# A graph-attention kernel with its slots laid out anew: score blocks and weighted sums in pairs, the dense work in one block, two small operations moved from VectorE to ScalarE

## Chip, cores and metric

One core of a Trainium2 chip. The metric is the device time of one execution in microseconds (us). Times are medians of several executions. Single executions of one kernel differ by up to 0.5%.

## The reference, cut to what matters

32 graphs of 512 nodes with 256 features go through two layers, each with a residual and a norm:

```python
# layer 0: masked attention (8 heads of 32) + feed-forward
allowed = (adj > 0) | (swapaxes(adj, 1, 2) > 0) | eye
attn = softmax(where(allowed, (q * scale) @ k.T, -inf));  ctx = attn @ v
x1 = layernorm(x + ctx @ Wo.T + bo)
ff = relu(x1 @ W1.T + b1) @ W2.T + b2
x  = layernorm(x + layernorm(x1 + ff))
# layer 1: masked attention alone, the mask is adj != 0 removed
x  = layernorm(x + (attn1 @ v1) @ Wo1.T + bo1)
```

All in float32.

## The kernel before

A graph and layer is one slot; 64 slots run one after the other. A slot works on eight blocks k of 128 keys x 4 heads x 512 queries (k = 0 to 3 are heads 0 to 3, k = 4 to 7 heads 4 to 7). These are the pieces that the argument touches (cuts marked):

```python
def scores(self, layer, k):                 # "S": four score matmuls, array form 32*128
    s = ps_s.tile([P, HPC, N], F32, tag="s")             # four PSUM banks, one buffer
    ...  # nc.tensor.matmul(s[:, j, :], kT, qT)
    p = work.tile([P, HPC, N], F32, tag="p", bufs=8)
    nc.scalar.activation(p, s, AF.Exp, scale=SCALE)      # "Exp"
def masked(self, layer, k):                 # "mask", on VectorE
    nc.vector.tensor_tensor(p, p, m[...].to_broadcast([P, HPC, N]), ALU.mult)
def product(self, k):                       # "P": weighted sum, array form 128*32, into psA
    ...
    if kc == NQ - 1:
        if hg == 0: self.tile("cT", [ND, N], bufs=1)     # context, ONE buffer
        nc.scalar.copy(self.cT[:, hg, :], self.acc[hg])
def pair(self, k):                          # p[k] += p[k+1], an accumulating DMA issued by GpSimd
    nc.gpsimd.dma_start(out=self.p[k], in_=self.p[k + 1], accum_op=ALU.add)
def fold(self, dst, a, b):                  # p[dst] = p[a] + p[b], on VectorE
def sums(self, k, hg, first, last):         # "R": row sums by TensorE, psR, form 128*32
```

Everything else on TensorE (projections, transposes, feed-forward, the masks of the next graphs) has the dense form 128*128; its results share two PSUM banks ("d") and mostly leave by ScalarE. In PSUM, masks of layer 0 (psM) left by VectorE and masks of layer 1 (psN) by ScalarE. In the names below, `project` is the output projection, `out0` and `out1` take the statistics for the norm after it, `norm1` to `norm4` apply the norms, and `hidden` and `mlp` are the two layers of the feed-forward. The slot beside a feed-forward began and went on like this:

```python
def slot_forward(g, layer, last, later, rest):
    g.scores(layer, 0)
    ...
    g.scores(layer, 1); g.masked(layer, 0)
    last.project(0, 0); last.project(0, 1); last.out0(0); last.out0(1)
    g.scores(layer, 2); g.masked(layer, 1); g.product(0); g.pair(0)
    g.query_key(layer, 1, 1)
    last.norm1(0); last.norm1(1); last.out0(2); last.out0(3)
    g.scores(layer, 3); g.masked(layer, 2); g.product(1)
    last.transpose(last.x1, 0); last.norm1(2); last.norm1(3)
    g.scores(layer, 4); g.masked(layer, 3)
    last.hidden(0, 0); last.hidden(0, 2)
    last.transpose(last.x1, 1); last.residual1()
    g.product(2); g.pair(2)
    g.scores(layer, 5); g.masked(layer, 4)
    last.hidden(0, 4); last.hidden(0, 6); g.product(3)
    ...
```

The order within each engine is the order of this program.

## Time and profile before

| | before |
|---|---|
| time | 3380.41 us (3379.92 to 3380.94, 3 runs) |
| TensorE busy | 98% |
| VectorE, ScalarE busy | 78%, 50% |
| slots O1, F1, F2, O2 | 40.2, 64.75, 64.0, 39.5 us; 16 groups of 208.4 us |
| mean granted TensorE clock | 0.997 |

A slot is measured from its S0 to the next S0. O1 is layer 0 of the first graph of a pair (beside it stand the last output projections of the pair before and the masks of the graphs to come), F1 layer 0 of the second graph (beside the feed-forward of the first), F2 layer 1 of the first, O2 layer 1 of the second. The prediction below shows the page's busy line and chain, and stretches of the timelines. The waits of TensorE (what waited, for what: us in total, times, longest), of the kernel before:

```profile
PE psS L273 <- ACT p L277: 13.4, 34, 1.0
PE psR L314 <- DVE p L307: 11.9, 31, 0.4
PE psA L290 <- DVE p L282: 5.7, 7, 4.0
```

TensorE waits almost nowhere: 31 us in the three largest entries. Next the view by windows, for one stretch of 3.41 us (the length, then the busy time of TensorE, its weight loads, VectorE, ScalarE and GpSimd, each with its number of instructions, then the granted clock, the DMA share and GB/s):

```profile
1021.83:1025.24 3.41, 3.41 (x21) 1.92 (x21) 2.96 (x3) 2.09 (x4) 0.38 (x1) 1.00 0.90 302
```

### The profile page before, as it was taken

The numbers are of one execution on the slowest core, as the hardware profiler recorded it, in microseconds if no ns is written. First come the engines' busy times: TensorE is split into PE (matmuls) and PEld (weight loads), VectorE is DVE, ScalarE is ACT, GpSimd is POOL, SyncE is SP. The second block draws the span as 40 slices with busy tenths as digits, with TensorE's granted clock in tenths as the row PEclk, the third lists the DMA queues.
The fourth block names the chain that finished last, engine by engine and source line by source line (L and its number), as shares of the span: only waits on it lengthen the run. The fifth ranks groups of instructions, "written<-read, shape, count | busy, mean of one in ns | idle before, by whom it ended". The sixth has DMA issues, their size and how long they took to land.

```text
span 3379.3 us, 47797 instructions
## 1 busy us (share of the span) xinstructions
PE 3321.8 (98%) x19210; PEld 1808.0 (54%) x19210; DVE 2620.6 (78%) x3525; ACT 1684.5 (50%) x1921; POOL 1111.7 (33%) x1641
## 2 busy tenths in 40 slices
PE   8999999999999999999999999999999999999997
PEld 3655546455464554645546455564655645555464
DVE  5787787878878777787777877778777787877877
ACT  4454454545545455454554544545445455444543
POOL 2333333233333333323333233332423323333232
PEclk9999999999999999999999999999999999999999
DMA  7454555545645455464554645536455365454643
GB/s 173 88 106 100 94 113 100 103 91 105 116 86 115 87 109 108 82 125 83 111 100 86 128 86 110 101 83 125 85 110 100 82 125 97 97 100 91 120 77 70
DMA packets 169670, 343.83 MB, mean 102 GB/s; under 512 B 10081, under 2 KB 144353, under 8 KB 144865
## 3 DMA queue, kind: packets, MB, share of 16 engines
q0 software_dynamic: 112128, 285.24, 46.9%
q1 hardware_dynamic: 57312, 55.46, 5.0%
q8 instruction: 153, 2.51, 0.3%
q14 instruction: 77, 0.62, 0.1%
HBM read 72.23 MB, written 16.78 MB: 26 GB/s over the span
## 4 chain that ended last, share of the span: by engine, by line
PE 85%; DVE 9%; ACT 4%; DMA 1%; issue 1%; POOL 0%; SPq 0%; POOLq 0%; DVEq 0%
PE psS L273 16%; PE psH L380 14%; PE psF L398 13%; PE psA L290 11%; PE psV L243 6%; PE psQK_None L260 6%; PE psO L359 6%; DVE p L282 4%; ACT p L277 4%; PE psQK L260 4%; PE psR L314 3%; PE psT L231 2%; DVE p L307 2%; PE psM L206 1%; PE psN L218 1%
## 5 line engine op out<-in xcount | busy, mean ns | idle before, releaser
L282 DVE TENSOR_TENSOR p<-p,m 128x2048 f32<-128x2048 f32 x512 | 1164.7, 2281 | 51.4 <-ACT p L277 51.3
L277 ACT ACTIVATE p<-psS 128x2048 f32<-128x2048 f32 x512 | 961.5, 1878 | 470.7 <-PE psS L273 433.6
L337 POOL TENSOR_SCALAR rs<-mv 128x1 f32<-128x1 f32 x512 | 376.4, 735 | 1223.9 <-DVE mv L336 1205.5
L273 PE MATMUL psS<-qT,kT 32*128 32x512 f32 x4096 | 583.9, 640 | 15.9 <-ACT p L277 13.4
L290 PE MATMUL psA<-p,v 128*32 128x512 f32 x4096 | 539.7, 605 | 5.7 <-DVE p L282 5.7
L380 PE MATMUL psH<-xT,w_L_gnn_W 128*128 128x256 f32 x2048 | 467.7, 384 | 0.0
L398 PE MATMUL psF<-w_L_gnn_W,hT 128*128 128x256 f32 x2048 | 455.9, 381 | 0.0
L380 PEld LDWEIGHTS psH<-xT,w_L_gnn_W 128*128 128x128 f32 x2048 | 381.2, 190 | 123.3 <-issue 51.1
L388 ACT ACTIVATE hT<-psH,c_L_gnn_b 128x256 f32<-128x256 f32 x512 | 214.6, 470 | 430.5 <-PE psH L380 429.4
L398 PEld LDWEIGHTS psF<-w_L_gnn_W,hT 128*128 128x128 f32 x2048 | 384.0, 190 | 73.9 <-ACT cT L300 24.3
L338 POOL TENSOR_TENSOR rs<-rs,neg_half 128x1 f32<-128x1 f32 x512 | 306.4, 598 | 42.7
L273 PEld LDWEIGHTS psS<-qT,kT 32*128 32x128 f32 x4096 | 159.9, 182 | 273.1 <-issue 199.4
L307 DVE TENSOR_TENSOR p<-p,p 128x2048 f32<-128x2048 f32 x128 | 292.6, 2286 | 4.1 <-DMA p<-p 1.8
L304 POOL DMA_DIRECT2D p<-p x192 | 182.3, 949 | 263.3 <-PE psV L243 174.9
L260 PE MATMUL psQK_None<-xT,w_L_gnn_Wqkv 128*128 128x512 f32 x512 | 254.6, 620 | 3.3 <-DMA w_L_gnn_Wqkv<-in_L_gnn_Wqkv_dram 3.3
L359 PE MATMUL psO<-w_L_gnn_Wo,cT 128*128 128x256 f32 x1024 | 248.6, 391 | 0.5 <-DVE held L829 0.5
L250 ACT COPY v<-psV 128x512 f32<-128x512 f32 x128 | 74.9, 585 | 347.6 <-PE psV L243 347.6
L359 PEld LDWEIGHTS psO<-w_L_gnn_Wo,cT 128*128 128x128 f32 x1024 | 188.0, 191 | 98.0 <-issue 63.3
L324 POOL TENSOR_TENSOR total<-total,sT 128x16 f32<-128x16 f32 x128 | 37.5, 293 | 574.8 <-DVE sT L321 574.8
L314 PE MATMUL psR<-p,ones 128*32 128x512 f32 x1536 | 198.0, 601 | 13.9 <-DVE p L307 11.9
L290 PEld LDWEIGHTS psA<-p,v 128*32 128x32 f32 x4096 | 84.0, 108 | 234.6 <-issue 84.8
L321 DVE STREAM_TRANSPOSE sT<-psR 128x512 f32<-128x512 f32 x128 | 91.5, 715 | 151.0 <-PE psR L314 151.0
(74 smaller groups left out, 3308.7 us busy)
## 6 DMA issues: line engine op xcount, KB each, us to landing
p<-p POOLq DMA_DIRECT2D x192, 1024.0 KB, 7.7
x<-in_x_dram SPq DMA_DIRECT2D x64, 512.0 KB, 4.3
x<-bov POOLq DMA_DIRECT2D x64, 512.0 KB, 5.8
adj<-in_adj_dram POOLq DMA_DIRECT2D x32, 512.0 KB, 6.9
x<-s_L_gnn_ln_b POOLq DMA_DIRECT2D x32, 512.0 KB, 7.9
x<-s_L_gnn_b POOLq DMA_DIRECT2D x32, 512.0 KB, 5.6
out_dram<-x SPq DMA_DIRECT2D x32, 512.0 KB, 3.0
w_L_gnn_W<-in_L_gnn_W_dram SPq DMA_DIRECT2D x2, 1024.0 KB, 12.6
```

Of the source, the lines that this page charges most:

```text
L260: nc.tensor.matmul(ps, w[:, i, c * P : (c + 1) * P], self.xT[:, i, at], start=(i == 0), stop=(i == ND - 1))
L273: nc.tensor.matmul(s[:, j, :], self.kT[at, hg, kc * P : (kc + 1) * P], self.qT[at, hg, :], start=True, stop=True)
L277: nc.scalar.activation(p, s, AF.Exp, scale=SCALE)
L282: nc.vector.tensor_tensor(p, p, m[:, k % NQ, None, :].to_broadcast([P, HPC, N]), ALU.mult)
L290: nc.tensor.matmul(self.acc[hg][j * HD : (j + 1) * HD, :], self.v[:, kc, h * HD : (h + 1) * HD], self.p[k][:, j, :], start=(kc == 0), stop ...
L307: nc.vector.tensor_tensor(self.p[dst], self.p[a], self.p[b], ALU.add)
L314: nc.tensor.matmul(self.total[j * HD : (j + 1) * HD, :], ones, self.p[k][:, j, :], start=first, stop=last)
L337: nc.gpsimd.tensor_scalar(rs, mv[:, 1:2], EPS, None, ALU.add)
L338: nc.gpsimd.tensor_tensor(rs, rs, neg_half[:, 0:1], ALU.pow)
L359: nc.tensor.matmul(ps[:, j, :], self.cT[:, k, at], wo[layer][:, k, :], start=(k == 0), stop=(k == ND - 1))
L380: nc.tensor.matmul(ps[:, j, :], w1[:, c, at], self.xT[:, c, h * 2 * P : (h + 1) * 2 * P], start=(c == 0), stop=(c == ND - 1),)
L398: nc.tensor.matmul(ps, self.hT[h][:, f, j * P : (j + 1) * P], w2[:, f, :], start=(f == 0), stop=(f == NF - 1))
```

## The change

The intent: a change of the array's form costs TensorE time, and in the kernel before it changed form 1781 times. So each slot is laid as four rounds of scores, a pair of weighted sums, scores, and one dense block. To relieve VectorE, the masks of layer 0 are taken by Sign on ScalarE, and the last norm is applied on ScalarE, with an offset -mean*rstd made on GpSimd. The core of the diff, with cuts marked:

```diff
-                nc.vector.tensor_scalar(self.m0[:, i, :], ps, 0.0, None, ALU.is_gt)
+                nc.scalar.activation(self.m0[:, i, :], ps, AF.Sign)
...
+                ms = small.tile([P, 1], F32, tag="ms", name=f"ms_{self.b}_{n}_{i}")
+                nc.gpsimd.tensor_scalar(ms, mv[:, 0:1], rs, -1.0, ALU.mult, ALU.mult)
+                return ms, rs
...
-                nc.vector.tensor_scalar(self.x2[:, i, :], y, mean, rs, ALU.subtract, ALU.mult)
+                nc.scalar.activation(self.x2[:, i, :], y, AF.Identity, bias=ms, scale=rs)
... opening of a slot that follows an O slot: P6, P7 and their row sums come from the slot before
+            elif last:
+                last.product(6)
+                last.product(7)
+                last.sums(3, 1, first=True)
+                last.sums(4, 1, last=True)
+            g.scores(layer, 1)
... F slots
             g.scores(layer, 2)
-            g.masked(layer, 1)
             g.product(0)
+            g.product(1)
             g.pair(0)
-            g.query_key(layer, 1, 1)
...
             g.scores(layer, 3)
-            g.masked(layer, 2)
-            g.product(1)
-            last.transpose(last.x1, 0)
             last.norm1(2)
             last.norm1(3)
+            g.masked(layer, 2)
+            g.masked(layer, 3)
+            g.query_key(layer, 1, 1)
...
+            last.transpose(last.x1, 0)
             g.scores(layer, 4)
-            g.masked(layer, 3)
-            last.hidden(0, 0)
-            last.hidden(0, 2)
+            g.product(2)
+            g.product(3)
+            g.scores(layer, 5)
+            g.masked(layer, 4)
+            g.masked(layer, 5)
             last.transpose(last.x1, 1)
             last.residual1()
-            g.product(2)
             g.pair(2)
-            g.scores(layer, 5)
...
+            for f in range(0, NF, 2):
+                last.hidden(0, f)
             last.mlp(0)
+            last.mlp(1)
             g.fold(2, 2, 0)
... O slots in the same way; the last graph's second projection now comes after S5 in O1:
+            g.scores(layer, 5)
+            g.masked(layer, 4)
+            if new:
+                new.value(0, 0)
+            if last and not forward:
+                last.project(1, 1)
```

## The prediction

> **What bounds the kernel now.** I read the page first (shares of the engines, then the chain that ended last), then the timelines of TensorE, VectorE and ScalarE over slots in the steady middle. The program is 64 slots. Each slot computes eight score blocks S0 to S7 of one graph and layer, their Exp, their masks and their weighted sums P0 to P7, and puts the dense work of another graph between them.
>
> ```profile
> PE 3321.8 (98%) x19210; PEld 1808.0 (54%) x19210; DVE 2620.6 (78%) x3525; ACT 1684.5 (50%) x1921; POOL 1111.7 (33%) x1641
> ...
> PE 85%; DVE 9%; ACT 4%; DMA 1%; issue 1%; POOL 0%; SPq 0%; POOLq 0%; DVEq 0%
> ...
> L282 DVE TENSOR_TENSOR p<-p,m 128x2048 f32<-128x2048 f32 x512 | 1164.7, 2281 | 51.4 <-ACT p L277 51.3
> L277 ACT ACTIVATE p<-psS 128x2048 f32<-128x2048 f32 x512 | 961.5, 1878 | 470.7 <-PE psS L273 433.6
> ...
> L307 DVE TENSOR_TENSOR p<-p,p 128x2048 f32<-128x2048 f32 x128 | 292.6, 2286 | 4.1 <-DMA p<-p 1.8
> ```
>
> TensorE is the bound: it is hardly idle and carries 85% of the chain. VectorE is second at 78%, so whether it delays TensorE is a matter of order, not of total.
>
> ```profile
> 1000.01 1.06 PE L290 MATMUL psA<-p,v 128*32 128x512 f32 x8
> 1000.89 1.04 PE L314 MATMUL psR<-p,ones 128*32 128x512 f32 x8
> 1001.87 7.17 PE L380 MATMUL psH<-xT,w_L_gnn_W 128*128 128x256 f32 x32
> ...
> 1036.35 1.07 PE L290 MATMUL psA<-p,v 128*32 128x512 f32 x8
> 1037.35 1.98 PE L260 MATMUL psQK_None<-xT,w_L_gnn_Wk 128*128 128x512 f32 x4
> ```
>
> The first column is the start. A weighted sum takes 0.88 us when a block of the same array form (128*32) follows, and 1.00 us when another form follows. Over all matmuls of the trace, the medians from start to start are: dense 256-column 216 ns, but 309 ns before another form; last matmul of a 128*32 block 409 ns, but 522 ns before another form. A score block takes 1.07 us whatever follows. So leaving the dense form costs 93 ns and leaving the 128*32 form 113 ns.
>
> Measured from each slot's S0 to the next one's, slots repeat in groups of four per pair of graphs: O1 40.2, F1 64.7, F2 64.0, O2 39.5 us (O: beside output projection and masks; F: beside the feed-forward); 16 groups of 208.4 us are 3334 us, and head and tail make the rest.
>
> **What the Trainium skill says.** "TensorEngine Tiling (Array Packing)", Key Properties: "Changing tiling mode (not just tile) drains the TensorE". The trace agrees, with 93 and 113 ns. "TensorE: Matmul & The Clock Gate", architectural detail on queue depths: matmuls and the instructions of ScalarE and VectorE keep their order, and only weight loads are pulled ahead. The trace agrees: VectorE sits idle 2.40 us in the next fence behind a psO that is not ready, though nothing else is missing. "ScalarE: Activation LUTs", What ACT_TABLE_LOAD costs: about 186 ns + 0.833 ns per element with immediates, for every function, and 93 ns more per pointer operand. The mask copy of layer 1 (128x512) takes 602 ns here, against 613 by that sum; so I take 0.60 us for Sign, and estimate 186 + 186 + 213 = 0.58 us for the norm with two pointers. The built program has one table load, as before.
>
> **The change, part by part.** The built order of TensorE's instructions holds the same matmuls, but 1117 changes of array form in place of 1781. Exits from dense fall from 759 to 319 (440 x 93 ns = 41 us), exits from 128*32 from 510 to 288 (222 x 113 ns = 25 us), exits from scores stay about 512. **Gain: 66 us, 4.1 us per group.** Sign and norm take 87 + 50 us from VectorE and put 77 + 74 us on ScalarE; neither is the bound, so only their place in the queues counts. P6, P7 and two row sums of a slot move to the next slot's opening: no work added.
>
> The cost is waits, since the regrouping asks for masked blocks sooner. I follow each slot in the built order with the durations above.
>
> F slots: VectorE must do, in this order, the statistics of out0(0), out0(1), mask 1, norm1, out0(2), out0(3), norm1, masks 2 and 3. Here is that stretch before, from the timeline of VectorE and then of TensorE:
>
> ```profile
> 1115.98 0.42 DVE L348 TENSOR_TENSOR y<-psO,x 128x256 f32<-128x256 f32 x1 [2.40 <-PE psO L359]
> ...
> 1117.98 2.27 DVE L282 TENSOR_TENSOR p<-p,m 128x2048 f32<-128x2048 f32 x1
> ...
> 1124.26 2.26 DVE L282 TENSOR_TENSOR p<-p,m 128x2048 f32<-128x2048 f32 x1
> ...
> 1128.53 4.49 DVE L282 TENSOR_TENSOR p<-p,m 128x2048 f32<-128x2048 f32 x2
> ...
> 1129.34 0.60 PE L231 MATMUL psT<-ident,x 128*128 128x128 f32 x4
> 1129.87 1.07 PE L290 MATMUL psA<-p,v 128*32 128x512 f32 x8
> 1130.87 1.14 PE L273 MATMUL psS<-qT,kT 32*128 32x512 f32 x8
> 1131.94 3.72 PE L380 MATMUL psH<-xT,w_L_gnn_W 128*128 128x256 f32 x16
> 1135.59 1.06 PE L290 MATMUL psA<-p,v 128*32 128x512 f32 x8
> ```
>
> From 1115.98 to the end of mask 3 (the first of the two at 1128.53) are 14.8 us without a gap; P3 came only at 1135.59, behind two pairs of hidden blocks (7.3 us) and S5. In the new order nothing of the feed-forward stands before P3. From the end of the first projection to P3, TensorE has: projection 1.73, S2 1.07, P0 and P1 1.88, S3 1.07, key projection 1.72, transposes 0.53, S4 1.07, P2 0.88 = 10.0 us, and in F1 a value projection more, 11.7. VectorE needs 15.2 (masks 2 and 3 now end together, so norm1(2) also waits about 0.4 for GpSimd's part). So TensorE waits **3.5 us in F1 and 5.2 us in F2**, shared between P1, P2 and P3. Further 0.3 us for a row sum on its fold and 0.5 us for the last transpose (one P fewer stands before it; the norm it needs ended just 0.5 us ahead of it before): 0.8 us each.
>
> Openings of O1 and F1: the row sum over the fold needs sums chain 2.5, masks 6 and 7 4.4, fold 2.3 after S7, 9.4 us with latency; TensorE has 8.4 between: **1.0 us** each, where 0.4 to 0.5 us were waited.
>
> O2: P1 needs two statistics and mask 1 (4.3 us) after the projection; TensorE has 2.55: 1.75. Masks now leave PSUM by ScalarE, in order with value and transpose copies, through two banks; the built bank numbers put a mask right behind the transpose of its own bank: 0.75 + 0.6. **3.1 us.**
>
> O1: the same bank waits 0.8, scores on Exp 0.3. The worst is the context copy (cT, one buffer): it follows P3, but the last graph's second output projection, now placed after S5, still reads the old one. The copy waits for that projection and stands in front of Exp 5 and the value copy in ScalarE's queue. From S5: projection ends 4.8, copy 5.4, Exp 7.3, value copy 7.8; only then a bank for the transposes, 8.3; two norms and its copy 9.5; three masks in turn to S6 at 11.4, against 6.1 us of work: 5.3. With the opening **7.4 us.**
>
> Sum per group: O2 3.1, O1 7.4, F1 1.0 + 3.5 + 0.8 = 5.3, F2 5.2 + 0.8 = 6.0: 21.8 us. Less the switches, 4.1, less waits of before that these replace (row sums on folds 1.3, scores on Exp 0.8): +15.6 us, x 16 = 250 us. The first slot has no predecessor and misses some: about -10. **3380 + 240 = 3620 us.**
>
> **The rivals.**
> - Switches alone count and the waits vanish: 3380 - 66 - some 30 of old waits = 3285 us. For it: TensorE is 98% busy and all 664 removed changes lie on it. Against it: VectorE's stretch of 14.8 us has no gap, and its order hasn't lost an instruction there.
> - Gain and waits cancel: only the F waits are real (8.7 x 16 = 139 us) and the O slots, which I worked out from bank numbers and queue places, lose little: 3380 + 139 - 66 = 3450 us. VectorE does lose 137 us of work, but in the O slots, where it had room.
> - A new bound on ScalarE: its total rises to 1836 us, 51%; only its order can hurt, as in O1. If TensorE's gaps also add weight loads not hidden (104 ns at a resumed block in the trace), or row sums wait for the pair DMAs (7.7 us median), it gets to 3700 us.
>
> **Range and chances.** The F waits are the surest, the O1 jam is next; the bank waits are loosest. Taking a third off or on to the 21.8 us of waits moves the time by 116 us; the errors are partly independent, so 3530 to 3710. Faster by over 2% needs under about 2 us of the waits per group to remain; same needs under about 11.
>
> **What would show it.** Right: matmul busy time falls while idle before psA on p (5.7 us in all before) rises to well over 100 us; F1 and F2 about 69 to 71 us, O1 about 45 us, O2 less than before by its moved work; long waits of the transposes in O1, with Exp 5 late behind the cT copy; VectorE about 137 us less busy. Wrong: F slots not longer than before, or P3 not waiting; the 128*32 exits not cheaper; or a time under 3450 us, which would mean that VectorE runs ahead of where I put it.

## The result and the profile after

The changed kernel takes **3758.82 us** (3756.06 to 3758.92, 4 runs), beside 3380.68 us for the kernel before in the same rounds; the ratio is 1.1117 (95% interval 1.1097 to 1.1136). A ratio is the mean time of one kernel's runs over that of the other's of the same rounds, so it is not quite the ratio of the medians. The prediction was 3620 us, with a range up to 3710: the direction was right, and the size was missed by 139 us. These lines of the page answer to those that the prediction shows:

```profile
PE 3398.0 (90%) x19210; PEld 1884.1 (50%) x19210; DVE 2498.7 (67%) x3269; ACT 1812.8 (48%) x2177; POOL 1105.3 (29%) x1769
...
PE 58%; DVE 22%; ACT 12%; POOL 3%; issue 3%; DMA 0%; DVEq 0%; ACTq 0%; POOLq 0%
...
L282 DVE TENSOR_TENSOR p<-p,m 128x2048 f32<-128x2048 f32 x512 | 1156.4, 2284 | 346.4 <-ACT p L277 346.4
L290 PE MATMUL psA<-p,v 128*32 128x512 f32 x4096 | 543.6, 636 | 141.8 <-DVE p L282 141.8
```

TensorE's share of the chain falls from 85% to 58%, and VectorE's rises to 22%, although VectorE has 122 us less to do. Nor is it saturated: it stands idle 346 us before masks, waiting for Exps, which in turn wait for scores. Engines wait for each other in turn. The same number of TensorE instructions is *busy* for 76 us more than before, though forms change less often; that was the first sign of a slower clock. The waits of TensorE, and one of ScalarE:

```profile
PE psA L290 <- DVE p L282: 141.8, 114, 2.8
PE psT L231 <- ACT v L250: 44.0, 15, 2.9
PE psS L273 <- ACT kT L263: 22.6, 47, 0.6
...
ACT cT L300 <- PE psO L364: 73.2, 15, 4.9
```

The first line is the F slots' masks (before 5.7 us), the second and the last are the jam in O1. The stretch of F2 that answers to the one in the prediction, on TensorE and then on VectorE (start, us, instruction, idle before and its releaser in brackets):

```profile
1085.52 1.07 PE L290 MATMUL psA<-p,v 128*32 128x512 f32 x8 [2.39 <-DVE p L282]
1087.72 1.94 PE L290 MATMUL psA<-p,v 128*32 128x512 f32 x8 [1.14 <-DVE p L282]
1089.59 2.09 PE L273 MATMUL psS<-qT,kT 32*128 32x512 f32 x8
1091.61 1.11 PE L231 MATMUL psT<-ident,x 128*128 128x128 f32 x4
...
1108.13 1.92 PE L290 MATMUL psA<-p,v 128*32 128x512 f32 x16
```

```profile
1083.18 6.69 DVE L282 TENSOR_TENSOR p<-p,m 128x2048 f32<-128x2048 f32 x3
1093.65 2.29 DVE L282 TENSOR_TENSOR p<-p,m 128x2048 f32<-128x2048 f32 x1 [3.79 <-ACT p L277]
...
1103.71 0.42 DVE L353 TENSOR_TENSOR y<-psF,x 128x256 f32<-128x256 f32 x1 [7.77 <-PE psF L403]
```

P2 waits 2.39 us and P3 1.14 us for masks that VectorE only now finishes, and a moment later VectorE itself idles 3.79 and 7.77 us. An undisturbed pair of weighted sums takes 1.92 us (the last line), but P3, S5 and the transposes behind the wait take nearly twice their time: 1.94, 2.09 and 1.11 us against 1.07, 1.14 and 0.60. Nothing waits in them. The clock does that, as the jam in O1 shows best. The timeline of TensorE there, from the transposes behind the second projection to S6:

```profile
976.33 0.66 PE L231 MATMUL psT<-ident,x 128*128 128x128 f32 x4 [2.93 <-ACT v L250]
977.79 0.59 PE L218 MATMUL psN<-ident_b,none 128*128 128x128 bf16 x4 [0.80 <-ACT xT L234]
...
980.53 2.09 PE L273 MATMUL psS<-qT,kT 32*128 32x512 f32 x8
```

The timeline of ScalarE in the same place:

```profile
973.43 0.59 ACT L300 COPY cT<-psA 128x512 f32<-128x512 f32 x1 [4.88 <-PE psO L364]
973.91 1.88 ACT L277 ACTIVATE p<-psS 128x2048 f32<-128x2048 f32 x1
975.68 0.59 ACT L250 COPY v<-psV 128x512 f32<-128x512 f32 x1
```

And the view by windows, with the columns as above:

```profile
974.32:977.74 3.42, 0.66 (x4) 0.48 (x5) 1.91 (x1) 3.42 (x5) 0.00 (x0) 1.00 0.01 0
977.74:981.15 3.41, 2.68 (x18) 1.94 (x21) 2.24 (x7) 1.53 (x3) 1.57 (x5) 0.50 0.00 0
981.15:984.56 3.41, 3.41 (x20) 0.59 (x16) 0.00 (x0) 2.02 (x2) 0.52 (x2) 0.50 0.00 0
```

ScalarE idles 4.88 us before the context copy, and Exp 5 and the value copy, for which the transposes wait, stand behind that copy. In the window from 974.32, TensorE is busy 0.66 of 3.42 us (19%), and in the next two the granted clock is 0.50. The clock records of all runs start and end on a fixed grid of 3.413 us. In this kernel, records at 0.50 ("low records", or half clock) fill 252.2 us, against 21.5 us before.

**Where the time went.** I compared every step from one matmul's start to the next one's with the undisturbed median of its kind. Per group of four slots, in us (waits are counted from start to start here, so they are a little over the idle times in brackets):

| | before | after |
|---|---|---|
| undisturbed work | 202.7 | 198.8 |
| waits, O1 / F1 / F2 / O2 | 0.8 / 0.4 / 0.4 / 0.8 = 2.4 | 7.8 / 5.2 / 6.6 / 5.5 = 25.2 |
| half clock, O1 / F1 / F2 / O2 | 0 | 2.7 / 0.1 / 2.8 / 0 = 5.6 |
| weight loads not hidden, rest | 3.3 | 2.5 |
| group | 208.4 | 232.1 |

The 16 groups make 16 x 23.7 = 379 us; 378 us were measured. The switches gained 3.9 us a group, as intended; the waits cost 22.8 us more, the half clock 5.6 us.

### The profile page after: what moved, and what is told of

The parts are those of the page before. It is cut to its first block, busy times and chain, and to the rows that moved or that the text cites. A ratio compares the mean times of both kernels' runs of the same rounds, so it can differ in the third digit from the quotient of the medians.

```text
span 3756.2 us, 48029 instructions
## 1 busy us (share of the span) xinstructions
PE 3398.0 (90%) x19210; PEld 1884.1 (50%) x19210; DVE 2498.7 (67%) x3269; ACT 1812.8 (48%) x2177; POOL 1105.3 (29%) x1769
## 4 chain that ended last, share of the span: by engine, by line
PE 58%; DVE 22%; ACT 12%; POOL 3%; issue 3%; DMA 0%; DVEq 0%; ACTq 0%; POOLq 0%
PE psH L385 12%; PE psS L273 11%; PE psF L403 9%; DVE p L282 8%; ACT p L277 8%; PE psA L290 5%; PE psR L314 5%; PE psQK_None L260 4%; PE psO L364 4%; DVE st L336 4%; PE psV L243 3%; DVE y L353 3%; PE psQK L260 2%; DVE p L307 2%; POOL rs L339 2%
## 5 line engine op out<-in xcount | busy, mean ns | idle before, releaser
L338 POOL TENSOR_SCALAR rs<-mv 128x1 f32<-128x1 f32 x512 | 260.8, 509 | 1352.0 <-DVE mv L337 1338.0
L273 PE MATMUL psS<-qT,kT 32*128 32x512 f32 x4096 | 614.8, 671 | 33.6 <-ACT kT L263 22.6
L385 PEld LDWEIGHTS psH<-xT,w_L_gnn_W 128*128 128x128 f32 x2048 | 390.5, 194 | 85.4 <-issue 24.3
L290 PEld LDWEIGHTS psA<-p,v 128*32 128x32 f32 x4096 | 102.6, 113 | 528.3 <-DVE p L282 255.8
L339 POOL TENSOR_TENSOR rs<-rs,neg_half 128x1 f32<-128x1 f32 x512 | 315.9, 617 | 42.7
L353 DVE TENSOR_TENSOR y<-psF,x 128x256 f32<-128x256 f32 x128 | 53.8, 420 | 387.9 <-PE psF L403 387.9
L304 POOL DMA_DIRECT2D p<-p x192 | 193.7, 1009 | 291.9 <-PE psA L290 283.8
```

The source lines that it names most:

```text
L273: nc.tensor.matmul(s[:, j, :], self.kT[at, hg, kc * P : (kc + 1) * P], self.qT[at, hg, :], start=True, stop=True)
L290: nc.tensor.matmul(self.acc[hg][j * HD : (j + 1) * HD, :], self.v[:, kc, h * HD : (h + 1) * HD], self.p[k][:, j, :], start=(kc == 0), stop ...
L338: nc.gpsimd.tensor_scalar(rs, mv[:, 1:2], EPS, None, ALU.add)
L339: nc.gpsimd.tensor_tensor(rs, rs, neg_half[:, 0:1], ALU.pow)
L385: nc.tensor.matmul(ps[:, j, :], w1[:, c, at], self.xT[:, c, h * 2 * P : (h + 1) * 2 * P], start=(c == 0), stop=(c == ND - 1),)
```

## The experiments

Each ran on the chip against the kernel before (3379.2 to 3381.6 us in all rounds). All results were correct.

### The two small swaps, without the new order

Edits to the kernel before, its order untouched: both swaps in the first run, then one each.

```diff
# Sign alone
-                nc.vector.tensor_scalar(self.m0[:, i, :], ps, 0.0, None, ALU.is_gt)
+                nc.scalar.activation(self.m0[:, i, :], ps, AF.Sign)
# the norm alone (with ms made by GpSimd in statistics(), as in the change)
-                nc.vector.tensor_scalar(self.x2[:, i, :], y, mean, rs, ALU.subtract, ALU.mult)
+                nc.scalar.activation(self.x2[:, i, :], y, AF.Identity, bias=ms, scale=rs)
```

> The kernel before with only the two engine swaps (Sign masks of layer 0 and the last norm on ScalarE), its order left alone. Theory (the new order costs, not the swaps): VectorE loses about 137 us of work and ScalarE gains about 130, neither is the bound, so 3340 to 3430 us. Rival (ScalarE's in-order queue becomes the new wait): over 3450 us, with TensorE waiting for ScalarE in the O slots.

> The kernel before with one edit: the masks of layer 0 are taken by Sign on ScalarE instead of by a comparison on VectorE; the order of the slots and the last norm stay. Theory (the loss of the run with both swaps in the old order comes from the last norm, which on ScalarE waits for GpSimd's product of mean and rstd behind a pair DMA issue): within 0.7% of before, 3365 to 3405 us; O1 slot 40.2 us within 1 us. Rival (masks leaving PSUM in ScalarE's order behind the Exps and copies are what costs): O1 rises by over 3 us, 3430 to 3500 us.

> The kernel before with one edit: the last norm of a layer-1 graph is applied on ScalarE with an offset made on GpSimd; order and masks of layer 0 stay. Theory (the norm on ScalarE waits some 10 us for GpSimd's ms, which stands behind a pair DMA in GpSimd's queue, and holds back every Exp behind it): carries most of the +181 us of the run with both swaps, 3500 to 3560 us, with low-clock windows; the wait of the norm on GpSimd of some 10 us in the waits of ScalarE. Rival (Sign masks carry the loss): within 0.7% of 3380 us.

Measured: both 3561.48 us, ratio 1.0535 (1.0518 to 1.0553), clock 0.987; Sign alone 3447.99 us, ratio 1.0197 (1.018 to 1.0214); the norm alone 3437.95 us, ratio 1.0169 (1.0152 to 1.0186). **Three misses.** In the first the rival came true: O1 went from 40.2 to 46.6 us and O2 from 39.5 to 44.6 us. By the 2% rule Sign alone is unclear and the norm alone the same, but both intervals lie clear of 1. The swaps are far from free in the old order: +66 us for Sign, +56 us for the norm, +180 us for both. The theory of the second run, that the norm carries the loss, fell; both carry about the same, and together more than their sum. The waits of TensorE with Sign alone, then with both, then a wait of ScalarE with both:

```profile
PE psT L231 <- ACT m L212: 34.7, 62, 0.6
PE psV L243 <- ACT m L212: 17.3, 31, 0.6
```

```profile
PE psT L231 <- ACT m L212: 75.7, 57, 2.9
```

```profile
ACT x L422 <- POOL ms L342: 94.2, 82, 10.5
```

With Sign alone, transposes and value projections wait 0.6 us at a time for a bank whose mask ScalarE hasn't yet taken: the masks stand behind Exps and copies there. 52 us of the 66 are these two lines. With the norm as well, ScalarE stops in places for GpSimd's offset, up to 10.5 us, and the masks now queue behind that stop too: the same wait of the transposes grows to as much as 2.9 us, and the clock drops (low records 97.6 us; half clock 2.2 us a group, about 35 us). What I gave as "neither is the bound, so only their place in the queues counts" was right as a sentence, but I then priced that place at nothing in the old order.

### The new order, without Sign

Edit to the kernel after:

```diff
-                nc.scalar.activation(self.m0[:, i, :], ps, AF.Sign)
+                nc.vector.tensor_scalar(self.m0[:, i, :], ps, 0.0, None, ALU.is_gt)
```

> The changed kernel with the masks of layer 0 back on VectorE (the norm stays on ScalarE, since with it on VectorE the new order deadlocks). Theory: the F slots stay at 72 us each, since no mask is built there, and the O slots shift by a few us either way: 3700 to 3830 us. Rival (Sign on ScalarE is what costs): under 3600 us.

Measured: 3766.55 us, ratio 1.1147 (1.1129 to 1.1166), slots 48.8, 72.7, 70.4, 40.1 us. As expected: in the new order Sign moves the time by 8 us only. So the order makes the loss, together with the norm that it needs on ScalarE; what that norm costs in the new order no run isolates. In the trace of the kernel after, ScalarE waits 15.1 us in all for GpSimd's offset, against 94.2 us with both swaps in the old order.

### A second buffer for cT

Edit: the kernel after with

```diff
-                        self.tile("cT", [ND, N], bufs=1)
+                        self.tile("cT", [ND, N], bufs=2)
```

(Room for it comes from sharing row constants that are equal in these inputs.)

> The changed kernel with two buffers for the context tile cT (room made by sharing bias and norm constants that are equal in these inputs). Theory: in O1 the copy no longer waits for the last graph's projection, so Exp 5 is not late: the 5.0 us of waits behind S5 in O1 fall to about 0.7 and the 2.7 us of half clock there vanish: 7 us x 15 slots = 105 us less, 3655 us, O1 about 41.6 us. Rival (the two PSUM banks alone cause those waits): at most 20 us less.

Measured: 3651.10 us, ratio 1.0799 (1.0781 to 1.0817). O1 falls from 48.6 to 42.5 us, its wait from 7.8 to 4.7 us and its half clock from 2.7 us to none; F2 changes by 0.8 us, F1 and O2 by under 0.1. The total is as expected, but not every part: of the 5.0 us behind S5 in O1, 1.9 us stay and not 0.7, and F2's gain was not in the sum. So the one buffer cost 108 us in all. Of it, 3.1 us x 15 slots = 47 us is the wait of the transposes behind the context copy, and 2.7 us x 15 = 40 us the half clock that came with it; F2's half clock lost 0.9 us a slot too.

### Useless matmuls in the gaps

Edit: the kernel after, with bf16 matmuls of 512 columns whose result nobody reads. In the first run 12 stand after O1's second projection, 8 before P2 and 3 before P3 in F2. In the others, 6 or 2 stand in O1 alone.

```diff
+            def fill(self, n):
+                ps = ps_a.tile([P, N], F32, tag="sum", name=f"psX_{self.b}")
+                for _ in range(n):
+                    nc.tensor.matmul(ps, ident_b, self.m1[:, 0, :], start=True, stop=True)
...
                 last.project(1, 1)
+                g.fill(12)
```

> The changed kernel with useless matmuls (bf16, 512 columns) put into two of TensorE's waits: 12 behind the projection in O1, 8 and 3 before P2 and P3 in F2. Results stay right. Theory (the clock is halved after a stretch with TensorE under half busy, and that costs 5.5 us per group on top of the waits): the half clock records vanish from O1 and F2, both slots fall by about 2.7 us: 3758 - 85 = 3675 us, in spite of more work. Rival (the slow matmuls behind the waits are part of the waits themselves): no gain, 3755 us or more.

> The kernel after with six useless matmuls (128x512 bf16, 0.23 us each) after the second output projection of O1, in the middle of its wait of 2.9 us. Theory (a window under about one half busy halves the clock of the next): the window of 19% busy in O1 gets to 0.19 + 6 x 0.226 / 3.413 = 0.59, so the half clock of O1 (2.67 us a slot) goes in most slots while the wait itself stays as long in sum with the filler: O1 about 46 us, total 3759 - 40 = about 3719 us (3710 to 3735). Rival (half clock follows from the longest gap or from the mean over longer stretches): O1 within 0.7 us of 48.6 us, total over 3745 us.

> The same with two useless matmuls in place of six. Theory: the window gets to 0.19 + 2 x 0.226 / 3.413 = 0.32, still well under the limit: O1 stays within 0.5 us of 48.6 us, half clock about 2.7 us a slot, total 3759 us within 12 us. Rival (any work in the gap keeps the clock up, since the longest gap falls from 2.9 to about 2.5 us): O1 about 46 us, total about 3719 us.

Measured: with 12 + 11, **3700.83 us**, ratio 1.0945 (1.0927 to 1.0963): adding work made the kernel 58 us faster. O1 falls from 48.6 to 46.0 us and F2 from 72.0 to 69.5 us, by nearly the half clock of each; F1 gains 1.6 us, where 13 windows of 35 to 44% busy now halve the clock: its waits hadn't changed, but they fell otherwise on the grid. This is why the gain is 58 us and not 85. With 6, 3757.08 us (1.1112, 1.1094 to 1.1131), a **miss**; with 2, 3755.12 us, as the theory expected (one execution of five took 3736.36 us, and it is the one that was profiled). The windows of O1 with 12, and then with 6 useless matmuls:

```profile
959.70:963.12 3.42, 2.27 (x14) 1.12 (x13) 2.11 (x1) 3.22 (x5) 0.00 (x0) 1.00 0.03 5
963.12:966.53 3.41, 2.73 (x29) 1.22 (x30) 2.05 (x7) 2.01 (x4) 1.76 (x5) 1.00 0.00 0
```

```profile
973.70:977.11 3.41, 0.97 (x8) 0.56 (x7) 2.02 (x1) 3.29 (x5) 0.00 (x0) 1.00 0.01 0
977.11:980.53 3.42, 2.73 (x18) 1.82 (x21) 2.13 (x7) 1.68 (x3) 1.69 (x5) 0.50 0.00 0
```

With 12 the window has 2.27 us busy (66%) and the next keeps its clock. With 6 it has 0.97 us (28%): most of the six had run before the window began, so my sum (19% + 40%) put them into the wrong window, and the next one is halved. The theory of the limit stands, and the placing on the grid was wrong.

So I counted over all 17 profiled runs, of both kernels and all experiments, leaving out the first and last eight windows of each and windows at half clock themselves. Of the windows in which TensorE's matmuls filled under 40%, 269 of 269 were followed by a window at half clock; between 40 and 50%, 80 of 206; over 50%, 1 of 16,653. That is a rule of share of busy time in a window of a fixed grid, not of the longest gap: the longest idle gap in O1 is 2.93 us, less than a window, and with 6 useless matmuls, where the clock was halved as well, it is 1.64 us. A recount over the windows at half clock gives the way back: under 80% busy, 148 of 149 were followed by another at half clock; between 80 and 90%, 23 of 51; over 90%, 1 of 133. A matmul takes about twice as long there, so 80 to 90% at half clock is the work of 40 to 45% at full clock. One limit on the work in a window would fit both counts; that is inferred, and no run isolates it.

### Can the F slots' waits be removed by order alone?

Five runs, each adding to the last. Edits to the kernel after, in the F slots unless said:

```diff
# hidden early: the four pairs of hidden blocks of the first half ahead of S4, P2 and P3
             last.transpose(last.x1, 0)
+            for f in range(0, NF, 2):
+                last.hidden(0, f)
             g.scores(layer, 4)
...
-            for f in range(0, NF, 2):
-                last.hidden(0, f)
# pair early: the DMA of blocks 2 and 3 ahead of the residual's DMA in GpSimd's queue
             g.product(3)
+            g.pair(2)
...
             last.residual1()
-            g.pair(2)
# both repairs: and cT with two buffers
# mask first: and mask 1 ahead of the second statistics (F), of both (O2)
             last.out0(0)
+            g.masked(layer, 1)
             last.out0(1)
-            g.masked(layer, 1)
# fold early: and the fold ahead of the feed-forward's statistics; hidden blocks behind S4
+            g.fold(2, 2, 0)
             last.mlp(0)
             last.mlp(1)
-            g.fold(2, 2, 0)
```

> The kernel after with one edit: in the F slots the four pairs of hidden blocks of the first half (14.6 us of dense work by the durations of the kernel before) stand before S4 instead of after S5, so that they lie in front of P2 and P3. Theory (the waits of P2 and P3 are VectorE's stretch of masks seen from an order that has too little dense work in front; no capacity is lacking): the waits of P2 and P3 (1.24 + 1.21 us in F1, 2.47 + 1.27 us in F2) go to under 0.3 us each, the half clock of F2 (2.8 us a slot) goes with them, F1 falls from 72.1 to about 69.5 us, F2 from 72.0 to about 65.5 us, O slots stay: about -9.4 us a group, 3759 - 150 = about 3610 us (3580 to 3650). Rival (VectorE lacks capacity in the F slots, so the wait only moves to the next block that VectorE feeds, P4 and P5, or to the second layer of the feed-forward): F slots stay within 1 us of 72 us, total above 3720 us.

> The run with the hidden blocks early, with one more edit: the pair DMA of blocks 2 and 3 is issued right after P3, ahead of the residual's DMA issue, behind which it stood in GpSimd's queue (GpSimd was idle 11.3 us there, waiting for the transposes of x1). Theory (the row sum's 4.1 and 3.8 us of wait and the half clock of some 1.9 us in that run come from the late pair DMA, which holds the fold and with it VectorE): the row sum's wait falls to under 1 us, the half clock of both F slots goes, F1 about 70.5 and F2 about 65.8 us, group 224 us, total 3630 us (3600 to 3665). Rival (VectorE's own work ahead of the fold is what lasts): row sum's wait stays over 2.5 us and the total over 3720 us.

> The run before with a second buffer for cT as well. Theory (the two largest waits of the changed order, O1's context copy and the F slots' masks, lie in different slots and add up): O1 falls from 48.3 to 42.5 us as it did alone (107 us saved there), total about 3525 us (3490 to 3560). Rival (they share VectorE or ScalarE, so that one repair uses up the other's gain): above 3580 us.

> The run before with mask 1 taken ahead of the statistics of the output projection in VectorE's order (ahead of the second one in F slots, of both in O2). Theory (P1's waits of 1.97 us in O2 and 0.8 us in F1 and F2 are VectorE's order alone): O2 falls from 39.5 to about 37.6 us, F slots by 0.7 us each, total about 3.3 us a group or 50 us less than the run before, about 3475 us (3435 to 3510), still above the kernel before. Rival (the statistics that now come later hold the norms and the transposes, so the wait only moves): within 15 us of the run before.

> The run with both repairs and mask 1 first, with two more edits in the F slots: the fold of blocks 2 and 4 stands ahead of the statistics of the feed-forward in VectorE's order (they wait 4.2 us for the residual's DMA, and the fold behind them), and S4 ahead of the first hidden blocks (which wait 0.9 us for the copy of the transposes). Theory (order alone): the row sum's wait of 2.95 us goes to under 0.5 us in both F slots, and with it their half clock of 1.3 us; F1 about 69, F2 about 64.5 us; the group about 214 us; total about 3480 us (3445 to 3520), against 3632 us. Rival (VectorE lacks the time; the wait moves to the norms, transposes or P6): over 3560 us.

Slots are medians without the first and last group:

| run | us | ratio (95%) | O1, F1, F2, O2 |
|---|---|---|---|
| hidden early | 3797.94 | 1.1231 (1.1212 to 1.1249) | 48.3, 76.1, 70.8, 39.5 |
| + pair early | 3741.11 | 1.1067 (1.105 to 1.1084) | 48.0, 73.3, 68.9, 39.5 |
| + second cT | 3653.06 | 1.0809 (1.0792 to 1.0826) | 42.5, 73.1, 68.4, 39.5 |
| + mask first | 3632.32 | 1.0749 (1.0732 to 1.0765) | 42.5, 73.5, 69.2, 38.4 |
| + fold early | 3462.32 | 1.0244 (1.0227 to 1.0261) | 42.5, 68.3, 64.3, 38.4 |

The first is a **miss** with the wrong sign. P2 and P3 no longer waited, as expected, but the row sum over the fold waited 4.1 and 3.8 us instead. GpSimd and, in the next run, VectorE show why:

```profile
1110.36 1.30 POOL L168 DMA_DIRECT2D x<-s_L_gnn_b  x1 [11.27 <-PE psT L231]
1111.12 1.44 POOL L304 DMA_DIRECT2D p<-p  x1
```

```profile
1095.73 0.42 DVE L353 TENSOR_TENSOR y<-psF,x 128x256 f32<-128x256 f32 x1 [4.22 <-DMA x<-s_L_gnn_b]
...
1097.74 2.27 DVE L307 TENSOR_TENSOR p<-p,p 128x2048 f32<-128x2048 f32 x1
```

In the first, the pair DMA (the last line) stands behind the residual's, for which GpSimd waits 11.27 us. With the pair DMA moved ahead, the wait of the row sum falls only to 2.9 us, not under 1: VectorE stands idle 4.22 us for the residual's transfer, with the fold behind it in its queue, whose operands are there for the last 3.1 us of this (the pair DMA landed at 1092.65). So this one missed in size too (3741 against an expected 3630 us): the rival's figures came true, but its cause, VectorE's own work, did not. The next missed as well (3653 against 3525 us): the second cT took off 88 us where 105 were expected. Mask 1 first removed P1's waits in both kinds of slot, but gave 21 us rather than 50: the F slots came only 0.4 to 0.5 us earlier to the row sum, whose wait stayed at 2.95 us, half clock in them grew from 2.0 to 2.4 us a group and the tail by 2.9 us, and in O2 a mask waited 1.55 us instead of 0.89.

The last run has both obstacles out of the way and is as expected (3462 against 3480 us). The waits of F1 and F2 are 1.3 and 1.5 us, low records 32.1 us in the whole kernel. VectorE is busy 2497.4 us, as in the kernel after. **So VectorE lacked no time; the order of three queues made the waits**, and each repair had only shown the next wait. What stays in this version is mostly in the O slots, 4.5 and 4.4 us a group: waits for ScalarE, of which this is the longest in the list of TensorE's waits.

```profile
PE psM L206 <- ACT xT L234: 31.8, 30, 1.4
```

With them it is still 2.4% over the kernel before.

### One idea of the change in the old order

Edits to the kernel before. In the first run P0 and P2 come one score block later, beside P1 and P3, and in the O slots P6 comes after a key projection, beside P7; shown for P0. In the second, only the last row sum of an O slot moves behind the next slot's S0:

```diff
# pairs
             g.scores(layer, 2)
             g.masked(layer, 1)
-            g.product(0)
-            g.pair(0)
...
             g.scores(layer, 3)
             g.masked(layer, 2)
+            g.product(0)
             g.product(1)
+            g.pair(0)
# the row sum later
             g.sums(4, 1, first=True)
-            g.sums(3, 1, last=True)
... at the start of the next slot
             g.scores(layer, 0)
+            elif last:
+                last.sums(3, 1, last=True)
```

> The kernel before with only one idea of the change taken: weighted sums run as pairs (P0 beside P1, P2 beside P3, P6 beside P7), by placing the first of each pair one score block later; dense work, masks and norms stay where they were and on VectorE. Theory (the exit cost of the 128*32 form is real, 113 ns each, and waits arise only where masked blocks are asked for sooner, which this order never does): about 13 exits fewer a group, -1.5 us a group, -24 us, about 3357 us (3340 to 3375), same by the 2% rule and faster by the interval. Rival (later products hold the p buffers longer, so scores and Exps wait for a free p): 3380 us or more, with waits of Exp for psA.

> The kernel before with one small idea of the change: the last row sum of the O slots (R over the fold of blocks 6 and 7) moves behind the next slot's S0, nothing else. Theory (the 0.49 to 0.57 us that this row sum waits for its fold in 32 slots is hidden by S0 at the price of one more exit of the 128*32 form, 0.11 us): -0.38 us x 32 = -12 us, about 3369 us (3358 to 3378). Rival (the normalization of cT comes later and holds the next slot's projection): 3385 us or more.

Measured: pairs 3416.18 us, ratio 1.0103 (1.0086 to 1.012), a **miss**. The row sum later: **3364.51 us**, ratio 0.9954 (0.994 to 0.9968), as expected, and the only version here that beats both kernels, though by 0.5% only. The waits of TensorE with pairs:

```profile
PE psR L314 <- DVE p L307: 32.1, 53, 2.0
PE psT L231 <- DVE m L212: 26.4, 31, 0.9
```

Pairs saved 1.3 us a group of form changes and added 3.9 us of waits. In O slots a weighted sum had stood between a mask and the transposes that reuse its bank; without it the transposes wait (0.9 us, 31 times). In the F slots the row sum waits longer for its fold. My rival (scores wait for a free p) isn't what happened either. Moving the one row sum took its wait for the fold (11.9 us in the kernel before) out of the list of waits, for one more exit of the form: O1 and F1 together went from 104.9 to 105.3 us, F2 and O2 from 103.5 to 102.0 us.

## Why the prediction was wrong

**Right: what bounds it, and the gain.** The matmuls' undisturbed work fell by 3.9 us a group against 4.1 predicted, by the count of form changes. Sign took 594 ns and the norm 601 ns on ScalarE, close to the 0.60 and 0.58 us that the prediction took for them.

**A wrong reading on the way.** The 2.40 us before 1115.98 do not show that VectorE keeps its order: the mask behind psO had its Exp only at 1115.96, so nothing there was ready to overtake. The fold that stood ready for 3.1 us in the run "pair early" shows it.

**Right: the F waits.** P1, P2 and P3 wait 3.2 us in F1 and 4.5 us in F2 (predicted 3.5 and 5.2); S4 in F2 waits 0.4 us more, but for ScalarE's copy of kT. That sum came from following VectorE's order against TensorE's.

**Right in kind: the jam in O1.** The transposes and the masks behind them wait 5.0 us (predicted 5.3), by the mechanism named. The second buffer for cT removes the 3.1 us of the transposes and leaves 1.9 us of the masks' waits.

**Failed: the sum had no term for the clock.** "Sum per group: ... 21.8 us. Less the switches, 4.1, less waits of before that these replace ...: +15.6 us, x 16 = 250 us" takes a wait to cost its own length. Where the jam of O1 and the waits of P2 and P3 in F2 left a window under about 40 to 50% busy, the work after it ran at half clock for one or two windows: 5.6 us a group, about 90 us, the larger part of the 139 us missed. The sign "matmul busy time falls" failed with it: it rose from 3321.8 to 3398.0 us. The Trainium skill, "TensorE: Matmul & The Clock Gate", Part 1, gives the 3413 ns of the free-running window, and this trace's grid of 3.413 us agrees. I cited that page for its queues and did not ask what the predicted gaps would do to the clock. Nor did any of my rivals include it; the one that reached 3700 us listed weight loads and pair DMAs, and neither grew (the table's row with the weight loads not hidden even fell, from 3.3 to 2.5 us a group).

**Mis-sized: the bank waits.** The waits came to 25.2 instead of 21.8 us a group, +54 us in all. The row sums on folds at the openings (1.0 us twice) nearly vanished (0.05 us in O1 and F1). In their place came waits of one kind that I had counted only in part, of TensorE for a result or a bank that ScalarE evacuates: the next slot's S0 on the copy of kT (0.62 us at the end of O1 and of O2), query and value projections on the copy of qT (0.45 us each), psF on the last relu (0.66 us in each F slot), psO in O2 (0.72 us). O2, predicted at 3.1 us, has 5.5 us of waits, so it kept its 39.5 us although 4.8 us of work had left it.

**Small: the tail.** The 10 us taken off for the first slot were right: it became 1.8 us shorter while the other O1 slots grew by 8.4. The sum had nothing for the tail, which grew from 56.0 to 65.3 us. Measured less predicted, the terms are: clock 90 us, waits 54, tail 9, smaller gain of the switches 3, old waits -5, weight loads and rest -13; together 138 of the 139 us.

**What stays open.** Between 40 and 50% busy the halving comes in 80 of 206 windows; the runs don't tell what decides there. Why 6 useless matmuls, or 2, leave the total within 4 us of the kernel after, though the wait changes its place on the grid, I only argue: the mean group there stays near 68 windows (232.1 us), as if a shift were given back at the next low window. The waits for ScalarE in the O slots (8.9 us a group in the last of the five runs, 142 us in all) are read from traces alone: no run removes them. Nor does a run tell the norm's part in the new order.

## What to carry to other kernels

A wait of TensorE costs its length only while the windows around it stay well over half busy; past that, add about half of the next window or two (2.7 us a slot here), and look at the clock by window as soon as the mean clock dips by a per cent. Before regrouping an order that has hardly a wait, follow each in-order queue past the first wait that you repair: here VectorE's masks hid a DMA issue behind another DMA, and that hid a fold behind a statistic, and a block that looks like a needless change of form may be what covers a bank's evacuation. Moving an operation to a less busy engine isn't free when TensorE waits for the bank that it empties.

## What the Trainium skill lacked or had wrong

- "TensorE: Matmul & The Clock Gate", HAM oscillation, gives as the abstract rule that TensorE should have no idle gaps over about 3.4 us, and the table of states in Part 1 an idle window (the page also tells of short, frequent idles that do it, without a share). Here the longest gap in O1 was 2.93 us, and windows up to 39% busy were always followed by half clock (269 of 269), windows of 40 to 50% in 80 of 206 cases, over 50% in 1 of 16,653. A share of busy time in a window describes these runs; an idle window or a gap of that length doesn't.
- The same table gives one busy window of about 3.4 us for the return to full clock, without a share. Of 38 low records in the kernel after, 30 lasted two windows (6.8 us); a first window filled 78% at half clock (977.74 in the fence above) was not enough there; over all runs windows at half clock kept it in 148 of 149 cases under 80% busy, and in 1 of 133 over 90%.
- "TensorEngine Tiling (Array Packing)", Key Properties, states the drain without a number: 93 ns on leaving the dense form and 113 ns on leaving 128*32 here, 5 ns on leaving the score form, and the gain by the count of changes came out as 3.9 us a group against 4.1.
